# One kernel, two issue orders: a Newton-type matrix square root and a spectral convolution on one core

## The chip, the core and the metric

The kernel runs on one core of a Trainium2 chip. A core has five engines with instruction streams of their own: PE (TensorE, matrix products into the PSUM banks), DVE (VectorE), ACT (ScalarE), POOL (GpSimd) and SP (SyncE, which issues transfers here). They meet through semaphores. The metric is the time of one execution on the device in microseconds (us); lower is better.

## The reference

Input x is 32 images of 32 channels of 128 x 128 in float32. Cut to what matters:

```python
def _L0_conv_ref(A):                       # per image and channel, 128 x 128
    Y = A / norm(A);  Z = I
    for _ in range(5):
        T = 0.5 * (3 I - Z @ Y);  Y = Y @ T;  Z = T @ Z
    return Y * sqrt(norm(A))

def _L1_conv_ref(x, weights1, weights2):
    f = fftn(x, axes=(2, 3)).real
    top = einsum('bixy,ioxy->boxy', f[:, :, :32, :32], weights1)
    bot = einsum('bixy,ioxy->boxy', f[:, :, -32:, :32], weights2)
    return ifftn(zeros with top and bot put back).real

x = x + _L0_conv_ref(_gn(x))               # _gn: group norm, 16 groups of 2 channels
x = x + _L1_conv_ref(_gn(x), weights1, weights2)
```

## The kernel before, in words

**Layer 0.** The work unit is a *quad*, four channels of one image, 256 in all. `prep` takes the statistics of an image or a pair of images (bn_stats, L207, on the tiles `xs`), and from them the scales and offsets of the group norm; `root` (L152 to L162) takes square roots, and its last use in `prep`, with the tag `a_t`, makes the scale `a_t_s` of layer 0's result. `staged` normalizes a quad's input in two layouts, on ACT (L342) and POOL (L349). `newton` computes the root as a polynomial iteration of two `quartic` rounds. Each step is four products of 128 x 128 on PE (`products`, L308), a transposition on PE (L314) or a wide product (L418), and after it an evacuation of the PSUM bank: q, v, w, t by `plus` on DVE (L283), my, mb, t, y on ACT (L407, L410, L275, L421, L424), r = mb + eye on POOL (L295, L302). In images 1 to 18 (`is_far`) the transposed w comes another way: DVE turns blocks of v (L374), a transfer writes them to DRAM and another reads them back (L376, L384, L387), and POOL adds r (L389).

**Layer 1.** `settle` stores a finished quad, folds it on POOL (L441) and takes its statistics on DVE (L446). `forward` and `spectrum` transform an image, `wide_products` (L617, group of 20 images), `small_products` (L687, groups of 7 and 3) and `last_products` (L732, group of 2) multiply by the weights, mode by mode, and `inverse` transforms back and writes out: products L870, copies to SBUF L876, products L888, then ACT copies L900, DVE additions L905 and the sums L838 in `unfold`. In the groups of 7, 3 and 2 images the loaded products are first put in another order (L858 on ACT; L853 on ACT and DVE for the last two images). The products of a group read buffers `diag` and `plain` that have zeros outside the blocks; they are cleared on POOL (L604, L673, L709) before the group's loads on SP (L591, L593, L651, L657).

**The order of the work.** All of this is Python generators. A main loop runs *rounds*: in each it advances nine lanes, each a quad in `newton`, by one step, and in between one step of `prep`, of the posts (`settle`, `forward`), the spectra, the products and the inverses. `rest` and `pause` are two empty steps between a result and its use. So the source's own order interleaves independent chains. A scheduler then takes the traced instructions: it issues, engine by engine, by priority and by its own reckoning of what is ready, unless an instruction is pinned. `kept` (L184) is the scheduler's pin: the instruction is put behind the one that the source has just before it on its engine. Before, it is on all transfers, on the normalizations of `staged` and on the products of `forward`; all the rest may move.

## Time and profile before

| | |
|---|---|
| three runs | 3047.10, 3047.77 and 3060.30 us; median 3047.77 |
| the profiled execution | 3058.61 us; its span, first to last instruction, 3056.7 |
| granted TensorE clock, mean | 0.978 |
| instructions | 73392 |
| DMA | 636.40 MB, 208 GB/s on average |
| PE, products L308 and L418 | L308 with w and v: 4096 records, mean 279 ns; L418: 2048 records, mean 383 ns |
| DVE, L283 q | 512, mean 680 ns |
| DVE, bn_stats L207 and L446 | 512 each, mean 412 ns and median 418 ns |
| POOL, L389 and L441 | 288, mean 1276 ns; 512, mean 734 ns |

An engine's busy time is the time in which one of its instructions runs. A float32 product on PE leaves two records. The idle time of a group is the time in which its engine stood still just before its instructions, and the releaser is what ended that. The end of a matmul in the profile is modelled.

### The profile page before, as it was taken

How to read it: one execution, taken by the hardware profiler on the slowest of the kernel's cores; microseconds unless marked ns; L12 is line 12 of the kernel's file. 1: busy time of each engine (PE TensorE's matmuls, PEld its weight loads, DVE VectorE, ACT ScalarE, POOL GpSimd, SP SyncE). 2: the span in 40 equal slices, each digit the busy share in tenths (PEclk: the TensorE clock that was granted, in tenths of full speed). 3: DMA queues.
4: the chain of work that ended last, by engine and by line, in shares of the span. 5: the costliest groups of instructions: out<-in, count | busy, mean ns of one | idle time of the engine just before them, and what ended most of it. 6: DMA issues, size and time to landing. Idle time of an engine off the chain costs nothing.

```text
span 3056.7 us, 73392 instructions
## 1 busy us (share of the span) xinstructions
PE 2901.3 (95%) x27076; PEld 2697.1 (88%) x27076; DVE 2238.3 (73%) x4255; ACT 1638.1 (54%) x4187; POOL 1999.1 (65%) x2312
## 2 busy tenths in 40 slices
PE   6999999999999999999999999999899998999994
PEld 6899999999999999999999888898898887888883
DVE  6778787878787878777866545777777765867664
ACT  3566566566565566565545544454454444555552
POOL 4577777776767777777755435676676763777452
PEclk9999999999999999999999999999999998999996
DMA  5476766767576768676733666677667667665675
GB/s 168 159 229 209 218 210 219 222 204 226 187 231 194 242 193 247 186 245 189 232 101 115 190 199 223 204 247 241 205 216 247 219 232 231 205 205 199 194 242 202
DMA packets 476659, 636.40 MB, mean 208 GB/s; under 512 B 97040, under 2 KB 257296, under 8 KB 476304
## 3 DMA queue, kind: packets, MB, share of 16 engines
q1 hardware_dynamic: 362976, 424.31, 43.3%
q10 hardware_dynamic: 113328, 207.41, 21.7%
q8 instruction: 217, 3.56, 0.5%
q14 instruction: 138, 1.13, 0.1%
HBM read 402.42 MB, written 229.11 MB: 207 GB/s over the span
## 4 chain that ended last, share of the span: by engine, by line
PE 76%; DMA 11%; DVE 5%; POOL 3%; ACT 2%; issue 2%; SPq 1%; ACTq 0%; DVEq 0%; POOLq 0%
PE ps L308 50%; PE ps L418 12%; PE ps L314 6%; DMA xs<-in_xs 4%; PE ps L464 2%; DMA w<-turn 1%; PE ps L888 1%; DMA or<-od 1%; PE ps L617 1%; POOL yt L838 1%; PE ps L870 1%; PE ps L529 1%; DVE yt L905 1%; DMA plain<-in_wk 1%; DVE a_st L207 1%
## 5 line engine op out<-in xcount | busy, mean ns | idle before, releaser
L308 PE MATMUL ps<-w,v 128*128 128x128 f32 x4096 | 555.8, 279 | 16.3 <-POOL w L389 6.6
L389 POOL TENSOR_TENSOR w<-w,r 128x512 f32<-128x512 f32 x288 | 366.6, 1276 | 306.5 <-DMA w<-turn 249.5
L342 ACT ACTIVATE b<-b,a_off,a_sc 128x128 f32<-128x128 f32 x1024 | 467.3, 490 | 160.4 <-issue 48.0
L308 PEld LDWEIGHTS ps<-w,v 128*128 128x128 f32 x4096 | 507.6, 194 | 29.2 <-POOL w L389 8.3
L418 PE MATMUL ps<-my,q 128*128 128x256 f32 x2048 | 491.6, 383 | 9.6 <-ACT d L900 6.0
L441 POOL TENSOR_TENSOR fold<-xt 128x256 f32<-128x256 f32 x512 | 364.6, 734 | 170.2 <-DVE xt L428 155.9
L283 DVE SCALAR_TENSOR_TENSOR q<-ps,eye 128x512 f32<-128x512 f32 x512 | 348.2, 680 | 164.4 <-PE ps L308 158.3
L838 POOL TENSOR_TENSOR yt<-yt,d 128x512 f32<-128x512 f32 x248 | 310.5, 1282 | 197.2 <-ACT d L900 150.6
L418 PEld LDWEIGHTS ps<-my,q 128*128 128x128 f32 x2048 | 370.5, 191 | 56.6 <-ACT d L900 6.8
L349 POOL TENSOR_SCALAR x<-xt,a_nm,a_sc 128x128 f32<-128x128 f32 x736 | 324.1, 455 | 18.6 <-DVE a_n L234 18.6
L302 POOL TENSOR_TENSOR r<-mb,eye 128x512 f32<-128x512 f32 x112 | 142.8, 1275 | 295.5 <-ACT mb L275 282.3
L421 ACT ACTIVATE t<-ps 128x256 f32<-128x256 f32 x512 | 192.8, 383 | 231.4 <-PE ps L418 226.5
L424 ACT ACTIVATE y<-ps,a_t_s 128x128 f32<-128x128 f32 x1024 | 312.0, 370 | 0.0
L207 DVE BATCH_NORM_STATS2 a_st<-xs 128x6 f32<-128x256 f32 x512 | 195.8, 412 | 139.1 <-DMA xs<-in_xs 138.6
L308 PE MATMUL ps<-y,t 128*128 128x128 f32 x2048 | 276.5, 279 | 10.4 <-DVE t L283 9.6
L308 PE MATMUL ps<-x,q 128*128 128x128 f32 x2048 | 278.2, 279 | 6.2 <-DVE q L283 6.2
L308 PE MATMUL ps<-x,b 128*128 128x128 f32 x2048 | 277.9, 279 | 5.9 <-POOL x L349 5.7
L407 ACT ACTIVATE my<-ps 128x512 f32<-128x512 f32 x256 | 152.9, 597 | 243.0 <-PE ps L308 238.0
L308 PE MATMUL ps<-my,mb 128*128 128x128 f32 x2048 | 277.3, 279 | 3.1 <-ACT d L900 3.1
L308 PE MATMUL ps<-my,q 128*128 128x128 f32 x2048 | 277.7, 279 | 2.1 <-ACT my L407 2.1
L308 PE MATMUL ps<-q,t 128*128 128x128 f32 x2048 | 275.2, 278 | 1.2 <-ACT d L900 1.2
L308 PEld LDWEIGHTS ps<-my,q 128*128 128x128 f32 x2048 | 262.4, 194 | 14.6 <-issue 2.7
(138 smaller groups left out, 5572.4 us busy)
## 6 DMA issues: line engine op xcount, KB each, us to landing
turn<-turn SPq DMA_DIRECT2D x288, 256.0 KB
b<-in_x ACTq DMA_DIRECT2D x256, 256.0 KB
xt<-in_xt ACTq DMA_DIRECT2D x256, 256.0 KB
xs<-in_xs ACTq DMA_DIRECT2D x256, 256.0 KB
mid<-xt SPq DMA_DIRECT2D x256, 256.0 KB
yt<-mid SPq DMA_DIRECT2D x128, 512.0 KB
out<-yt SPq DMA_DIRECT2D x117, 512.0 KB
w<-turn SPq DMA_DIRECT2D x144, 256.0 KB
```

What stands on the lines that cost most here:

```text
L207: nc.vector.bn_stats(st[:, 2 * k + j, :], tiles[k][:, j, :])
L283: nc.vector.scalar_tensor_tensor(s, ps, f, t, ALU.mult, ALU.add)
L308: nc.tensor.matmul(ps[:, j, :], lhsT[:, j], rhs[:, j], start=True, stop=True)
L314: nc.tensor.transpose(ps[:, j, :], t[:, j, :], ident)
L342: nc.scalar.activation(t, x, AF.Identity, bias=offset[:, c], scale=scale[:, c])
L349: nc.gpsimd.tensor_scalar(m[:, j, :], xt[:, j, :], nm[:, c // 2 : c // 2 + 1], sc[:, c : c + 1], ALU.add, ALU.mult,)
L389: nc.gpsimd.tensor_tensor(w, w, r, ALU.add)
L418: nc.tensor.matmul(both[j // 2][:, j % 2], q[:, j], my[:, j], start=True, stop=True)
L421: nc.scalar.mul(w[:, 2 * h : 2 * h + 2, :], both[h][:, :, 1, :], 1 / (MS * QF))
L424: nc.scalar.mul(y[:, j, :], both[j // 2][:, j % 2, 0, :], sn[:, c : c + 1])
L441: nc.gpsimd.tensor_tensor(f[:, :, 64 * half : 64 * half + 64], xt[:, :, 0:64], xt[:, :, 64:128], op)
L838: engine.tensor_tensor(yh, yh, d, op)
```

## The change

Every engine is wrapped. Each instruction that the kernel issues through `nc` is pinned behind the one before it on its engine, so that all five streams stand in the order of the source. `kept` becomes a function that returns its argument, as the wrapper does its work already. The building of the identity (`make_identity`) goes on by the unwrapped handle. The result of the last root of layer 0 (`a_t_s`) gets three buffers in place of two. In a profile, an instruction issued through the wrapper shows the wrapper's line.

```diff
+class InOrder:
+    def __init__(self, tc):
+        self.tensor, self.vector, self.scalar, self.gpsimd, self.sync = (
+            Engine(tc, getattr(tc.nc, n)) for n in ("tensor", "vector", "scalar", "gpsimd", "sync")
+        )
+
+class Engine:
+    def __init__(self, tc, engine):
+        self.tc, self.engine = tc, engine
+
+    def __getattr__(self, name):
+        issue = getattr(self.engine, name)
+        def issued(*args, **kw):
+            return self.tc.keep_in_program_order(issue(*args, **kw))
+        return issued
...
-    nc = tc.nc
+    nc = InOrder(tc)
...
-    make_identity(nc, ident)
+    make_identity(tc.nc, ident)
...
-        s = small.tile([P, n], F32, tag=f"{tag}_s", name=f"{tag}_s", bufs=2)
+        s = small.tile([P, n], F32, tag=f"{tag}_s", name=f"{tag}_s", bufs=3 if tag == "a_t" else 2)
...
-    kept = tc.keep_in_program_order
+    def kept(issued):
+        return issued
```

## The prediction

> **What bounds the kernel now.** I read the engine totals first, then the 40 slices, then the same busy times for four stretches of the span.

> ```profile
> PE 2901.3 (95%) x27076; PEld 2697.1 (88%) x27076; DVE 2238.3 (73%) x4255; ACT 1638.1 (54%) x4187; POOL 1999.1 (65%) x2312
> ...
> PE   6999999999999999999999999999899998999994
> ...
> 0.00:200.00 200.00, 167.54 (x1334) 158.83 (x1335) 141.01 (x300) 100.40 (x251) 109.94 (x142) 0.98 0.54 173
> 200.00:1700.00 1500.00, 1494.24 (x12513) 1416.34 (x12512) 1196.06 (x2299) 881.93 (x2288) 1062.53 (x1197) 1.00 0.66 204
> 1700.00:2900.00 1200.00, 1133.48 (x12154) 1031.36 (x12153) 817.21 (x1503) 595.66 (x1506) 758.48 (x905) 0.97 0.67 217
> 2900.00:3057.00 157.00, 106.00 (x1083) 90.53 (x1081) 84.06 (x155) 60.12 (x145) 68.18 (x69) 0.82 0.68 225
> ```

> The columns are stretch, length, then busy time of PE, PEld, DVE, ACT and POOL, the granted clock, DMA share and GB/s. PE is the bound. Its idle time is 3056.7 - 2901.3 = 155.4 us: 32 us in the first 200 us (the start), 6 us in the next 1500, 67 us from 1700 to 2900 (where layer 1's products and inverse run beside layer 0), 51 us at the end. So the change can matter in two ways only: it shortens these 155 us, or it makes PE wait at new places.

> **The change part by part.** The lists of the built programs show which instructions move. SP's 1962 transfers stand in source order before and after. Of PE's 14,562 instructions, neighbours are out of order at 8 places, in the first round and around the small products (L687). ACT has 335 such places of 4973, POOL 310 of 2309, DVE 1011 of 4255. So PE keeps its order, and the question is whether its inputs come later or earlier. From the end of the input's last producer to the start of the product that reads it, the trace has a median of 3.3 to 5.4 us for every operand of the iteration (w from POOL 3.9, q 3.9 to 4.3, v 3.3) and a fifth percentile of 0.8 to 2.3. Shifts below 1 us are covered by that; larger ones are not.

> *(a) The copies L858.* The inverse of the images of groups 1 and 2 copies its loaded products on ACT and multiplies them on PE in the same step of the source. Before, most of these copies were issued 20 to 30 us early:

> ```profile
> 2599.24 2.01 ACT L858 COPY ob<-or 128x1024 f32<-128x1024 f32 x1
> ...
> 2621.33 1.65 ACT L342 ACTIVATE b<-b,a_off,a_sc 128x128 f32<-128x128 f32 x4 [0.36 <-issue]
> 2622.01 1.16 PE L870 MATMUL ps<-tab,ob 64*128 64x128 f32 x16
> ```

> The second copy (2599.24) feeds the products at 2622.01. In source order it stands behind the four L342 that end at 2622.98. The copy then ends at 2625.0, and PE, which reads nothing else first, waits 3.0 us. I did the same for all ten: end of the ACT instruction ahead in source order, plus 2.0 us, less the start of L870. The first copy of each group was late already and stays. The other eight give 3.0, 0, 2.7, 1.9, 3.0, 3.9, 2.7 and 3.0: 20 us. Nothing hides it but PE's own idle time, 6 us of 200 there. Bounds: 0 (ACT always ahead of PE) and 8 x 4 = 32. I take +20.

> *(b) The clears L604, L673, L709.* Before, POOL cleared the buffers of the products 53 us to over 600 us ahead; now each clear stands at the head of its stage, and the loads on SP wait for it, with all that SP has behind them.

> ```profile
> L604 POOL MEMSET diag<- x2: 1802/1804/1805, 1647.2 to 1650.4; 128x2048 f32 x2
> L604 POOL MEMSET plain<- x2: 943/944/944, 1652.1 to 1653.0; 128x1024 f32 x2
> ...
> 1696.87 3.35 SPq L591 DMA_DIRECT2D diag<-in_wk  x4
> 1700.25 1.27 POOL L302 TENSOR_TENSOR r<-b,eye 128x512 f32<-128x512 f32 x1 [0.63 <-POOL x L349]
> 1700.55 0.35 SPq L593 DMA_DIRECT2D plain<-xs  x1
> 1705.62 1.11 PE L617 MATMUL ps<-diag,plain 128*32 128x128 f32 x32 [1.01 <-DMA diag<-in_wk]
> ```

> POOL's instruction ahead in source order is the L302 that ends at 1701.5. Two clears of 1.80 and one of 0.94 end at 1706.1, so the load L593 goes out 5.5 us later than 1700.55, and the product, which waits for its loads already, starts 5.5 us later. For the small products I do the same. The first clear of the first stage ends at 2482.2 where its spectra went out from 2480.4 on, with products at 2486.4: 0 to 1.8, I take 1. In the second stage 2827.3 stands against 2826.1: 1.2. L709 moves by about 2 us, with 100 us until its buffers are used: 0. Together +8. Bounds: 0, and 16, the sum of the clears (5.5 + 3 x 3.6).

> *(c) The end.* The last image's two copies L853 ran on idle engines; in source order they follow image 30's evacuations.

> ```profile
> 3029.47 1.05 ACT L853 COPY ob<-or 128x512 f32<-128x512 f32 x1 [2.26 <-DMA or<-od]
> ...
> 3034.77 1.53 PE L870 MATMUL ps<-tab,ob 64*128 64x128 f32 x16
> ...
> 3039.35 0.97 ACT L900 COPY d<-ps 128x256 f32<-128x256 f32 x3 [0.34 <-DVE yt L905]
> ```

> The L900 end at 3040.3; the copy ends 1.05 later, at 3041.4, 6.6 us after 3034.77. Some returns, because the next product (L888 at 3040.86) had waited 4.6 us for ACT's other copies. +4, bounds 0 and 7.

> *(d) POOL's w (L389) behind r (L295).* Before, w stood ahead of an r that the source has first in 162 pairs, and POOL then stood waiting for w's transfer:

> ```profile
> L389 POOL TENSOR_TENSOR w<-w,r 128x512 f32<-128x512 f32 x288 | 366.6, 1276 | 306.5 <-DMA w<-turn 249.5
> ...
> PE ps L308 <- POOL w L389: 6.6, 3, 4.2
> ```

> Now r, 1.28 us, fills part of that wait and w comes later by what is left. I put POOL's rows in source order with their durations, and their inputs at the times at which they arrived. This makes w 1 us late on average, and where slack is short PE is late by 20 us in all. The turning transfer starts sooner in return: in the same accounting for DVE, L374 comes 0.4 us earlier, because bn_stats L446 (0.42 us each, 411 of 512 ran ahead of source order) no longer stand before it. Bounds -6 (the 6.6 us go away) and +20; I take +8.

> *(e) Order on DVE and ACT otherwise.* In favour: going through PE's waits of 0.3 us and more and adding up what had overtaken the late producer on its engine gives 22 us at most. Against: an instruction that waits now holds all behind it; the same accounting makes PE later by 20 us on DVE, over the accounting for the old order. I take -10, bounds -22 and +20, nearer the gain, because q, v, t and w themselves come 0.1 to 0.4 us earlier in it.

> *(f) The third buffer* of the root adds no instruction. The scale of an image pair is rewritten only once its last reader is done; before, the shortest distance was 1.0 us: 0.

> [...] The trace shows L870 at 2.08 us after 11.59 us idle against 1.16 at 2622.01. [...]

> **Sum.** 20 + 8 + 4 + 8 - 10 = +30 us on a span of 3056.7: 3087. The profiled execution took 3058.6, 10.8 us over the median of the runs, so I carry the difference to the median: 3047.8 + 30 = 3078. The ends of all bounds are -28 and +95; both at once is unlikely on either side.

> **The rivals.**
> 1. *The source order feeds PE better.* POOL and ACT no longer stand in front of transfers (249.5 us at L389, 23.2 at L858) and the critical instructions pass the statistics. Against: PE had only 6 us of idle between 200 and 1700 to give. It decides if (a) stays under 10 us and (e) reaches its 22: 3047.8 - 22 - 6 + 4 (half of b) + 4 (c) = 3028. Chance 0.22.
> 2. *Nothing is seen.* PE's order is the same and its slack of 4 us takes up the rest; losses in (a) come back as shorter waits later. Within 0.5% (15 us, about what a measurement can tell) of 3048: say 3052. Chance 0.18.
> 3. *One blocked head holds everything.* DVE waits 138.6 us for xs at L207 before; if such waits, with yt at L905, now stand before q and v all through 1700 to 2900, PE's 67 us of idle there double: 3078 + 67 = 3145. Against: L207 hardly moves in the lists. Chance 0.10.
> 4. *The wrapper misses calls.* It can't: all lists of after ascend in source order, but for one constant. Chance 0.

> The forecast itself has 0.50. Faster 0.22, within 0.5% 0.18, slower 0.60. The range runs from 3026, (e) at its good end and nothing lost elsewhere, to 3128: (a) and (c) as taken and the bad ends of (b), (d) and (e), 20 + 4 + 16 + 20 + 20 = 80.

> **What would show it.** L870 of the images 21 to 26, 28 and 29 waits 2 to 4 us for ob; the first L617 waits some 6 us for its loads; PE is 98 to 100% busy from 200 to 1700 still; POOL's idle before w falls below 250 us; DVE's bn_stats of xt come later. I am wrong if ACT reaches the copies before PE does, or if the stretch from 200 to 1700 loses more than 25 us.

## The result and the profile after

The changed kernel took 3069.23 us (median of 8 runs, 3062.66 to 3074.93), the kernel before beside it 3048.22 (8 runs, 3045.40 to 3060.30). The ratio is 1.0065, 95% interval [1.0048, 1.0083]: some 20 us slower, where 3078 was predicted. The total came out right, but two of its terms were off by 20 us and more, in opposite directions, so part of that is luck. That shows only where PE is followed through the stages.

The profile page of the changed kernel, engine totals and the 40 slices of PE:

```profile
span 3064.9 us, 73467 instructions
...
PE 2897.2 (95%) x27076; PEld 2689.8 (88%) x27076; DVE 2244.1 (73%) x4255; ACT 1644.0 (54%) x4187; POOL 1997.2 (65%) x2312
...
PE   6999999999999999999999999999999998899984
```

Its busy times by stretch, in the columns that the prediction explains:

```profile
0.00:200.00 200.00, 167.12 (x1333) 159.30 (x1334) 145.82 (x301) 99.93 (x251) 109.07 (x141) 0.99 0.55 173
200.00:1700.00 1500.00, 1471.63 (x12234) 1387.62 (x12233) 1179.17 (x2239) 865.33 (x2246) 1042.13 (x1172) 1.00 0.65 201
1700.00:2900.00 1200.00, 1146.68 (x12383) 1046.57 (x12382) 829.24 (x1554) 613.75 (x1537) 773.43 (x929) 0.98 0.68 220
2900.00:3065.00 165.00, 111.78 (x1132) 96.31 (x1131) 89.86 (x164) 64.95 (x154) 72.54 (x73) 0.82 0.66 216
```

From 200 to 1700 PE now stands still for 28 us (6 before). From 1700 to 2900 it stands still less, 53 us (67 before), and its clock is 0.98 against 0.97. So the stage that was full has lost and the stage with gaps has won.

How much, and where, comes from the starts of the same product in both traces, as PE issues its products in the same order in both:

| stretch, in times of before | delay of after at its end, us | change, us |
|---|---|---|
| 0 to 200 | 0 | 0 |
| 200 to 1570 | +32 | +32 |
| 1570 to 1870, the first L617 in it (1705.6) | +36 | +4 |
| 1870 to 2670 | -12 | -47 |
| 2670 to 2771, copies L858 | +2 | +14 |
| 2771 to 3056.7 | +8 | +6 |

The two profiled executions are only 8 us apart, the medians 21: that of before (3058.6) is 10 us over its median. So the single stretches are good to about 10 us, and the sizes are taken from the runs below. How far one execution can be trusted shows in four of them that have the same order up to 1620 (this one, e4, e6 and e7 below): their delays there are 32, 29, 44 and 36 us.

*The loss from 200 on: w behind a waiting r.* Groups of the page of after; all wrapped instructions show line L83, so they are told by their tiles:

```profile
L83 POOL TENSOR_TENSOR r<-mb,eye 128x512 f32<-128x512 f32 x256 | 326.5, 1275 | 431.6 <-ACT mb L83 413.3
...
L83 PE MATMUL ps<-w,v 128*128 128x128 f32 x4096 | 557.0, 279 | 34.3 <-POOL w L83 26.0
...
L83 POOL TENSOR_TENSOR r<-b,eye 128x512 f32<-128x512 f32 x256 | 326.4, 1275 | 214.7 <-ACT b L83 160.4
...
L83 POOL TENSOR_TENSOR w<-w,r 128x512 f32<-128x512 f32 x288 | 365.1, 1275 | 121.0 <-DMA w<-turn 94.8
```

POOL's idle time before w fell from 306.5 to 121.0 us, as predicted, but POOL did not stop waiting: it waits before r instead, for ACT's mb and b. The two groups of r here hold all images. By line, in the repetition e4_all_lines below, the r of images 1 to 18 (L295) has 201.5 us of idle time before it where it reads b and 112.4 where it reads mb, 314 together; the kernel before has 40. The other r (L302), with 319.6 us where it reads mb, belongs to images whose w does not run on POOL, and had 295.5 before. PE pays with 26.0 us of waits for w (6.6 before). Of 35 such waits, counted from 0.02 us up, 29 come where POOL had stood still before an r among the three instructions ahead of that w. One such place, in the timeline of after:

```profile
554.00 0.48 ACT L83 ACTIVATE b<-b,a_off,a_sc 128x128 f32<-128x128 f32 x1
...
554.61 1.27 POOL L83 TENSOR_TENSOR r<-b,eye 128x512 f32<-128x512 f32 x1 [3.65 <-issue]
...
555.84 2.50 POOL L83 TENSOR_TENSOR w<-w,r 128x512 f32<-128x512 f32 x2
...
557.17 1.16 PE L83 MATMUL ps<-w,v 128*128 128x128 f32 x8 [1.26 <-POOL w L83]
```

POOL stands for 3.65 us until ACT has normalized b, then runs r, and only then w, for which PE waits 1.26 us.

*The step at the first L617: clears ahead of loads.* Timeline of after:

```profile
1732.73 3.55 POOL L83 MEMSET diag<- 128x2048 f32 x2
...
1736.22 1.84 POOL L83 MEMSET plain<- 128x1024 f32 x2
...
1737.19 0.34 SPq L83 DMA_DIRECT2D plain<-xs  x1
...
1740.16 1.94 PE L83 MATMUL ps<-diag,plain 128*32 128x128 f32 x32 [3.60 <-DMA plain<-xs]
```

The load goes out (1737.19) only when the first clear of `plain`, 0.95 us from 1736.22 on, is done, and PE waits 3.60 us for it. The delay steps from +31.9 at 1670 to +37.4 at 1719. Only 2.6 us of this step are the later start of this product (+34.5, against 1705.62 before); the rest comes in 6.83 us at half clock from 1739.40 on.

*The copies.* Timeline of after, the products L870 of four images (start, duration, and in brackets PE's wait):

```profile
2613.36 2.08 PE L83 MATMUL ps<-tab,ob 64*128 64x128 f32 x16 [2.88 <-ACT ob L83]
...
2682.30 1.16 PE L83 MATMUL ps<-tab,ob 64*128 64x128 f32 x16 [2.60 <-ACT ob L83]
...
2750.54 1.94 ACT L83 COPY ob<-or 128x1024 f32<-128x1024 f32 x1
2752.53 1.25 PEld L83 LDWEIGHTS ps<-tab,ob 64*128 64x128 f32 x16 [3.71 <-ACT ob L83]
2752.53 1.54 PE L83 MATMUL ps<-tab,ob 64*128 64x128 f32 x16 [3.31 <-ACT ob L83]
```

PE waits for the end of the copy. The nine waits add up to 26.4 us (two waits and 5.9 us before). The same 16 products take 1.16 us after one wait, at a granted clock of 1.00 (2682.30), and 2.08 after another, at 0.50 (2613.36); the last section returns to that.

*The gain from 1870 on: DVE no longer stands in front of a transfer.* Timeline of the kernel *before*, the same stretch on three engines:

```profile
2323.83 0.68 DVE L283 SCALAR_TENSOR_TENSOR v<-my,ps 128x512 f32<-128x512 f32 x1
2329.41 0.43 DVE L207 BATCH_NORM_STATS2 a_st<-xs 128x6 f32<-128x256 f32 x1 [4.90 <-DMA xs<-in_xs]
2329.75 1.87 DVE L905 TENSOR_TENSOR yt<-ps,yt 128x512 f32<-128x512 f32 x3
2331.54 0.68 DVE L283 SCALAR_TENSOR_TENSOR w<-ps,r 128x512 f32<-128x512 f32 x1
...
2330.46 0.97 ACT L900 COPY d<-ps 128x256 f32<-128x256 f32 x3 [5.89 <-DVE yt L905]
...
2330.88 1.46 PE L418 MATMUL ps<-my,q 128*128 128x256 f32 x4 [3.55 <-ACT d L900]
```

The statistic L207 at 2329.41, which the source has later than the L905, the w and the L900 around it, stands at the head of DVE and waits 4.90 us for xs. Behind it wait L905, w, ACT's L900 (for L905) and PE (for the bank that L900 empties). The scheduler had issued 399 of the 512 L207 ahead of something that the source has earlier. From 1850 to 2650, the group of L207 in the kernel before:

```profile
L207 DVE BATCH_NORM_STATS2 a_st<-xs 128x6 f32<-128x256 f32 x128 | 49.6, 415 | 69.4 <-DMA xs<-in_xs 69.3
```

and in the changed kernel:

```profile
L83 DVE BATCH_NORM_STATS2 a_st<-xs 128x6 f32<-128x256 f32 x128 | 47.5, 413 | 4.6 <-DMA xs<-in_xs 4.5
```

The wait of 69.3 us is gone; whether that is the gain, the experiments tell.

### The profile page after: what moved, and what is told of

The parts are those of the page before. It is cut to its first block, busy times and chain, and to the rows that moved or that the text cites. A ratio compares the mean times of both kernels' runs of the same rounds, so it can differ in the third digit from the quotient of the medians.

```text
span 3064.9 us, 73467 instructions
## 1 busy us (share of the span) xinstructions
PE 2897.2 (95%) x27076; PEld 2689.8 (88%) x27076; DVE 2244.1 (73%) x4255; ACT 1644.0 (54%) x4187; POOL 1997.2 (65%) x2312
## 5 line engine op out<-in xcount | busy, mean ns | idle before, releaser
L83 PE MATMUL ps<-my,q 128*128 128x128 f32 (+1 forms) x4096 | 734.5, 329 | 3.2 <-DVE w L83 1.5
L83 PEld LDWEIGHTS ps<-my,q 128*128 128x128 f32 x4096 | 625.6, 191 | 61.1 <-issue 6.8
L83 POOL TENSOR_TENSOR r<-mb,eye 128x512 f32<-128x512 f32 x256 | 326.5, 1275 | 431.6 <-ACT mb L83 413.3
L83 PE MATMUL ps<-w,v 128*128 128x128 f32 x4096 | 557.0, 279 | 34.3 <-POOL w L83 26.0
L83 PEld LDWEIGHTS ps<-w,v 128*128 128x128 f32 x4096 | 504.9, 193 | 53.9 <-POOL w L83 34.9
L83 ACT ACTIVATE b<-b,a_off,a_sc 128x128 f32<-128x128 f32 x1024 | 469.6, 493 | 150.9 <-issue 45.8
L83 DVE SCALAR_TENSOR_TENSOR q<-ps,eye 128x512 f32<-128x512 f32 x512 | 350.9, 685 | 225.5 <-PE ps L83 219.8
L83 ACT ACTIVATE my<-ps 128x512 f32<-128x512 f32 x512 | 306.4, 603 | 377.9 <-PE ps L83 361.7
L83 POOL TENSOR_TENSOR r<-b,eye 128x512 f32<-128x512 f32 x256 | 326.4, 1275 | 214.7 <-ACT b L83 160.4
L83 POOL TENSOR_TENSOR fold<-xt 128x256 f32<-128x256 f32 x512 | 363.6, 732 | 128.5 <-DVE xt L83 126.6
L83 POOL TENSOR_TENSOR w<-w,r 128x512 f32<-128x512 f32 x288 | 365.1, 1275 | 121.0 <-DMA w<-turn 94.8
L83 POOL TENSOR_TENSOR yt<-yt,d 128x512 f32<-128x512 f32 x248 | 310.8, 1279 | 147.7 <-ACT d L83 110.4
L83 ACT ACTIVATE t<-ps 128x256 f32<-128x256 f32 x512 | 191.4, 381 | 373.4 <-PE ps L83 361.5
L83 POOL TENSOR_SCALAR x<-xt,a_nm,a_sc 128x128 f32<-128x128 f32 x736 | 322.6, 451 | 18.6 <-DVE a_n L83 18.6
L83 ACT ACTIVATE y<-ps,a_t_s 128x128 f32<-128x128 f32 x1024 | 290.4, 374 | 0.0
L83 PE MATMUL ps<-y,t 128*128 128x128 f32 x2048 | 276.9, 279 | 8.1 <-DVE t L83 5.8
L83 PE MATMUL ps<-x,b 128*128 128x128 f32 x2048 | 277.3, 279 | 5.7 <-POOL x L83 5.7
L83 PE MATMUL ps<-x,q 128*128 128x128 f32 x2048 | 275.7, 278 | 3.2 <-DVE q L83 3.2
L83 PE MATMUL ps<-my,mb 128*128 128x128 f32 x2048 | 276.9, 279 | 0.0
L83 PE MATMUL ps<-q,t 128*128 128x128 f32 x2048 | 274.8, 277 | 0.5 <-DVE u L83 0.5
L83 DVE STREAM_TRANSPOSE turn<-v 128x512 f32<-128x512 f32 x288 | 264.8, 919 | 9.9
L83 PEld LDWEIGHTS ps<-y,t 128*128 128x128 f32 x2048 | 254.8, 194 | 13.0 <-issue 6.6
```

What stands on the lines that cost most here:

```text
L83: return self.tc.keep_in_program_order(issue(*args, **kw))
```

## The experiments

All variants have the third buffer. Where an order is pinned, the same relation as in the change is added to the traced instructions of the named engines, so that the lines stay readable. Ratios are to the kernel before, run on the same chip (medians 3050.77 beside e1 to e4, 3049.08 beside e5 to e8 and 3052.90 beside e9 to e12); 1% is 30.5 us.

**One engine at a time, and all.**

```diff
+    in_order(('DVE',))                      # e1_dve
+    in_order(('Activation',))               # e2_act
+    in_order(('Pool',))                     # e3_pool
+    in_order(('PE', 'DVE', 'Activation', 'Pool', 'SP'))   # e4_all_lines
```

> Only DVE's stream stands in source order; ACT, POOL, PE and SP are as in the kernel before (third root buffer kept). Theory: what the changed kernel wins between the first inverse and image 24 (47 us by matching PE's products in the two traces: 27 us of PE idle time and 19 us of half-clock windows) comes from DVE's order, because statistics and additions no longer run ahead of q, v, t and w. Then about 3005 us (ratio 0.986). Rival A: it comes from ACT's order; then 3048 +- 8. Rival B: it needs DVE and ACT in order together; then 3048 +- 8 here and for ACT alone.

> Only ACT's stream in source order. Theory: the copies of the loaded products (L858) now stand right before the products that read them, PE waits for them 26 us in place of 6, nothing else changes: 3068 us (ratio 1.0065). Rival A (ACT's order also gives the 47 us of the middle): about 3021. Rival B: about 3068 as the theory; e1 then tells.

> Only POOL's stream in source order. Theory: w (L389) stands behind r (L295), which waits for ACT, and PE falls back by 32 us up to image 19; the clears (L604) cost 5.5 us more: 3048 + 37 = 3085 us (ratio 1.012). Rival: w is late only because ACT in order brings b and mb later, so POOL alone costs just the clears: 3054 (1.002).

> The changed kernel itself, pinned by a pass at the end of the trace instead of by a wrapper, so that each instruction keeps its own line in the profile: the same streams, 3069 us (ratio 1.0065) by every theory. It is the reference of this set, and shows by line what POOL's w and r wait for.

| run | median, us | ratio [95%] | in us |
|---|---|---|---|
| e1_dve | 3020.84 | 0.9892 [0.9874, 0.9911] | -33 |
| e2_act | 3077.63 | 1.0090 [1.0061, 1.0118] | +27 |
| e3_pool | 3064.47 | 1.0039 [1.0023, 1.0055] | +12 |
| e4_all_lines | 3071.44 | 1.0068 [1.0046, 1.0089] | +21 |

e4 repeats the changed kernel. The change is three changes: DVE's order wins, ACT's and POOL's lose. DVE's gain is three times the predicted one, though less than the 3005 expected of e1. ACT's loss goes with the copies: from 2570 to 2980, in times of before, PE stands still 16 us longer in e2. No run has ACT alone in order with the copies moved. PE's waits in e2:

```profile
PE ps L870 <- ACT ob L858: 25.5, 9, 3.7
PE ps L870 <- ACT ob L853: 17.8, 2, 11.5
```

POOL was expected at 3085 and reached 3064: that one missed. Its profile loses 21 us up to 1516 and wins 26 back after 1850. PE's idle time differs by 4 us there; it is the half clock that differs: from 1870 to 2980 the profiled execution of e3 has 17 us of it, that of before 72, and half of the difference is 27 us. That of e3 is the fastest of its nine (3057.30), that of before is 10 us over its median, so part of this is the choice of the executions. The three single effects add up to +6 against +21 together; the intervals reach 5 to 9 us to either side, so this hardly proves an interplay.

**Undoing one cost at a time, all five engines in order.** e5 makes r inside the quartic (ahead of its use, for images 1 to 18 behind the empty steps, after mb has long come), e6 puts one step between a copy and its products, e7 clears early, with further steps in the products' generators to find the room, e8 is all three.

```diff
-        ready.append((xt, m, mb, plus_eye(mb, is_far(b), has_more(b, g))))
+        ready.append((xt, m, mb))
...
             yield from rest
+            r = plus_eye(mb, far, more)
             w = four("w", more)
...
                     obs[b].rearrange("p (l t o) -> p o t l", l=4, t=8),
                 )
+            yield
...
-        for t in diags + plain:
-            nc.gpsimd.memset(t, 0.0)
...
+        for t in diags:
+            nc.gpsimd.memset(t, 0.0)
+        yield
```

> All five streams in source order, but the source makes r = mb + eye a rest (two rounds) later, inside the quartic, so that POOL reaches it when ACT has long written mb or b, and w no longer stands behind a waiting r. Theory (POOL's head-of-line wait at r makes w late): PE's waits for w fall from 26 us to under 8, and the 30 us lost up to image 19 come back: 3070 - 28 = 3042 us (ratio to before 0.998). Rival (w is late because of its own transfer or of POOL's load, 65% busy): PE's waits for w stay above 18 us, 3062 to 3070 us (1.005 to 1.007).

> All in source order, but in the inverse the copy L858 or L853 and the products L870 that read it are one step of the source apart. Theory: PE's waits for L858 fall from 26 us to under 4 and the time by about 20: 3050 us (ratio 1.001). Rival (the loss returns as other waits, for the inverse's own chain gets one step longer for 12 images): 3065 to 3075 us (1.006 to 1.009).

> All in source order, but the buffers of the products are cleared when they are made or a step after the last product of the group before, as the scheduler had it, not at the head of their own stage. Theory: only the first L617 gets back its wait, about 5.5 us: 3064 us (ratio 1.005). Rival (the clears hold SP's queue and with it later transfers): up to 15 us, 3055 us (1.002).

> All in source order with the three edits of e5, e6 and e7 together: r later, the copy a step ahead, the clears early. If the costs are separate, as the theory has it, they add: 3070 - 28 - 20 - 6 = 3016 us (ratio 0.990), below both the kernel before and the changed one, since DVE's gain stays. Rival (the costs hide behind one another): 3030 to 3045 us (0.994 to 0.999).

| run | median, us | ratio [95%] | against e4, us |
|---|---|---|---|
| e5_r_later | 3037.50 | 0.9964 [0.9948, 0.9980] | -32 |
| e6_copy_step | 3037.94 | 0.9961 [0.9948, 0.9973] | -33 |
| e7_clear_early | 3082.63 | 1.0120 [1.0094, 1.0147] | +16 |
| e8_three_edits | 3033.43 | 0.9949 [0.9934, 0.9964] | -36 |

e5 isolates r ahead of w. PE's waits for w in e4_all_lines:

```profile
PE ps L308 <- POOL w L389: 26.5, 31, 2.4
```

and in e5_r_later:

```profile
PE ps L308 <- POOL w L390: 7.2, 6, 2.4
```

At 1620 it is 9 us behind the kernel before, where e4 is 29 behind. Later runs make this firmer: the four executions with r ahead of w (the changed kernel, e4, e6 and e7) are 29 to 44 us behind at 1620, the four with r moved (e5, e8, e9 and e10) 2 to 9, though the other edits of e6 to e10 come into play later. So term (d) is some 30 us there, and 32 in the medians at the end. e6, expected at 3050, takes eight of the nine waits for L858 away (26.3 us in e4; one of 2.2 us is left in e6) and wins 33. From 2570 to 2980 it is 36 us shorter than e4: 22 of them are idle time of PE, and 10 are the clock, as it has 10 us at half rate there in place of 31. e7 missed. The step at the first L617 is smaller (+1.6 in place of +5.5), but e5, which leaves the clears where they are, has +1.4; and e7 loses about 7 us near 2200 and 6 near 2500, where the added steps move the inverses against the rest; it mixes two things and says little about clears. Its loss is inside e8 as well. e8 missed the 3016 of separate costs: it is 36 us below e4, where its three parts by themselves add up to 49.

**Only what has no side effect, and the end.** e9 has e5, e6 and the first clear (L604) moved to where `change` is entered, with no step added for it. e10 also issues image 31's copies L853 together with image 30's.

```diff
+        for t in diags + plain:            # in change(); gone from the wide products
+            nc.gpsimd.memset(t, 0.0)
...
+            if more:                       # e10 alone
+                load_products(b + 1)
+                for k in (b, b + 1):
...
+                    for h, copy in enumerate((nc.scalar.copy, nc.vector.tensor_copy)):
```

> Everything in the order of the source, with r made behind the rest, a step between the copy L858 and the products L870, and the first clear (L604) moved up to where change() is entered, with no other step shifted. If the three costs are separate, they come off one by one from the 3071 of e4_all_lines: 33 (r, e5_r_later), 33 (copies, e6_copy_step) and about 5 (first clear): 3001, a ratio of 0.985, with the delay against the kernel before near +9 at 1620, no step at the first L617, and about -65 at the end. If the costs hide behind one another (time won in the first layer's stage is given back in the second by whatever is next, as e8_three_edits hinted), 3015 to 3030, a ratio of 0.990 to 0.995.

> e9_three_fixed with the copies L853 of image 31 issued together with those of image 30, so ahead of image 30's last evacuations. If the last wait of the products for DVE ob (6.6 us) is a cost of its own, 4 to 6 us below e9_three_fixed; if what follows in the tail is set by the last loads and stores anyway, within 2 us of it.

e9: 3011.91 us (3003.61 to 3016.17), ratio 0.9870 [0.9842, 0.9898]; 60 us below e4, of 71 if all were separate. Its median lies above the 3001 of separate costs and below the rival's 3015 to 3030, nearer to neither for certain, as the interval is 9 us to either side. The delay against the kernel before is +2.3 at 1652, +1.6 at 1859, -54.0 at 2662, -55.7 at 2973: the first stage and the copies cost next to nothing now, and the gain of the middle stays. What follows gives 8 back, PE's wait in the tail being longer (11.6 and none before):

```profile
PE ps L872 <- ACT ob L854: 19.6, 1, 19.6
...
PE ps L872 <- DVE ob L854: 6.2, 1, 6.2
```

e10: 3008.14 us, ratio 0.9861 [0.9827, 0.9895]. The wait for DVE ob is gone from its list, but the profiled span is 3011.9 against 3009.2, and the intervals overlap almost whole. What remains in the tail is a wait of 18.8 us for ACT ob, and ACT had itself stood 10.34 us for the load of `or`. Whether e10 gains 4 us can't be told from these runs.

**Where DVE's gain comes from.** e11 is the kernel before with only the statistics pinned (L207, shown, and L446 in the same way), e12 is e1 with r made later.

```diff
-                nc.vector.bn_stats(st[:, 2 * k + j, :], tiles[k][:, j, :])
+                kept(nc.vector.bn_stats(st[:, 2 * k + j, :], tiles[k][:, j, :]))
```

> The kernel before with the third buffer, and of all instructions only the statistics L207 and L446 kept in the order of the source on DVE. If what DVE's order wins (e1_dve, -33) is that statistics no longer run ahead of the roots' and evacuations' work, 3018 to 3025, a ratio of 0.990 to 0.993, with the delay against the kernel before turning from about +5 to below -20 between 1817 and 2620. If the gain is in the order of the other DVE operations (q, v, t, w, the preparations), 3045 to 3052, a ratio within 0.3% of 1.

> Only DVE in the order of the source (as e1_dve, 3021), with r made behind the rest as in e5_r_later. If the +10 that e1_dve shows at 1817 comes from r ahead of w, about 3010, a ratio of 0.986, with the waits of L308 for POOL w at 7 us or less, from 14.3; if those 10 us come from DVE w (11.8 us in e1_dve), no change: 3018 to 3023.

e11: 3017.65 us (3012.26 to 3030.47), ratio 0.9902 [0.9864, 0.9941], -30 us: as much as the whole order of DVE in e1, with 1024 pinned instructions. The delay goes from +6 at 1859 to -34 at 2559. The two rows of DVE from 1850 to 2650 and of PE's clock that go with it, in e11:

```profile
L207 DVE BATCH_NORM_STATS2 a_st<-xs 128x6 f32<-128x256 f32 x128 | 47.7, 412 | 2.9 <-DMA xs<-in_xs 2.8
```
```profile
1850.00:2650.00 800.00, 768.86 (x7653) 702.40 (x7653) 609.42 (x1128) 415.56 (x1069) 571.63 (x669) 0.99 0.72 237
```

and in the kernel before:

```profile
1850.00:2650.00 800.00, 747.89 (x7279) 681.14 (x7278) 573.22 (x1065) 392.19 (x1015) 540.40 (x631) 0.96 0.69 227
```

In 800 us PE is busy 21 us more, at 0.99 of its clock in place of 0.96. So the gain is that statistics no longer run ahead; the order of q, v, t and w among themselves is not needed for it. L207 and L446 were not pinned apart; the waits are L207's.

e12: 3038.18 us, ratio 0.9962 [0.9946, 0.9979]. Neither reading expected it to be slower than e1. PE's waits for w are the same (13.7 us, 14.3 in e1): so moving r in the source changed nothing in them while POOL's order is the scheduler's. Why e12 is 17 us above e1 stays open; its delay is +12 at 457 already, where e1 has +3, and a change of the source gives the scheduler other orders on all engines that are not pinned.

## Why the prediction was right, point by point

**(a) Copies, +20: right in its mechanism, short by the clock.** For the eight copies behind the first of their group PE waited 2.88, 0.03, 2.60, 2.46, 3.31, 3.69, 2.53 and 3.31 us, where 3.0, 0, 2.7, 1.9, 3.0, 3.9, 2.7 and 3.0 were forecast; the two first ones waited 5.6 us, 5.9 before. That is the forecast nearly copy by copy. The step that fell short: it has no term for the clock. Six of the nine waits were followed by a granted clock of 0.50, five times for 3.41 us and once for 6.83; half of these 23.9 us is 12 us, an estimate. Taking the waits out won 33 us (e6).

**(b) Clears, +8: the first number was met by luck.** The step of 5.5 us at the first L617 is there, but it is made up otherwise. The load L593 went out 4.7 us later against the products around it (5.5 forecast), and the product only 2.6. The forecast took it that the product "waits for its loads already", but the wait of 1.01 us was for `diag`; the load of `plain` had, by these figures, some 2 us to spare. The other 2.9 us come in the half clock behind it. Nor does the step belong to the clears alone: with the clears early, as in the kernel before, e2, e11 and e12 show 4.3, 3.0 and 3.2 us there and e10 shows 3.2; with the clears at the head of the stage e5 shows 1.4. So the 0.1 of e9 does not size the clear, and the small ones were not isolated either (e7).

**(c) The end, +4: the wait is there, its price is not settled.** Timeline of after:

```profile
3043.95 1.11 ACT L83 COPY ob<-or 128x512 f32<-128x512 f32 x1
3044.50 1.45 DVE L83 COPY ob<-or 128x512 f32<-128x512 f32 x1
...
3046.09 2.08 PE L83 MATMUL ps<-tab,ob 64*128 64x128 f32 x16 [6.60 <-DVE ob L83]
```

The wait is the 6.6 us of the forecast; the whole tail moved by about 2 us.

**(d) r ahead of w, +8: right in its mechanism, mis-sized beyond its bound of 20.** The trace of after shows 32 us lost from 200 to 1570, and moving r away wins 32 (e5). As far as the runs show, the step that failed is the discount from the 20 us of the accounting to 8, because the turning transfer "starts sooner in return". With DVE alone in source order PE's waits for w did not fall, they rose from 6.6 to 14.3 us (e1); and with POOL alone in order the delay at 1516 is 21 us (e3), near the 20 without the discount. The accounting also took the inputs "at the times at which they arrived". If w is late on PE, mb and b may come late from ACT in turn; that was not tested. The own words "if the stretch from 200 to 1700 loses more than 25 us" came true here. In the medians POOL's order by itself costs 12 us, clears and all (e3).

**(e) Order on DVE and ACT otherwise, -10: mis-sized, beyond its bound of -22.** e1 and e11 give -33 and -30. The step that failed counted what had *overtaken* a late producer, by its busy time. A statistic that overtakes costs 0.41 us of work, but it also stands and waits for its transfer, 69 us from 1850 to 2650. The clock had no term either: from 1870 to 2500 the profiled execution of after is 44 us shorter than that of before, 26 of them idle time of PE and 17 from 34 us less at half clock; as that of before is 10 us over its median, the clock's part may be smaller in the medians. The reason given against rival 3, that "L207 hardly moves in the lists", was wrong: 399 of 512 did. Rival 3's blocked head was there, but in the kernel before.

**(f) The third buffer** is in all variants alike; it was not tried by itself.

By engine the forecast was ACT +24 (a and c), POOL +16 (b and d) and DVE -10; the engines one at a time gave +27, +12 and -33. By themselves ACT and POOL were sized well, and DVE was wrong by 23 us. Together they came to +21 and not +6; why is open, if it is more than noise. In company (d) was too small by 24 us and (a) by 13, and (e) by 23 the other way. That these cancel as far as they do is luck, and they are not separate costs: 33, 32 and -33 alone add up to 32, more than the 21 us measured. Rival 1, the source order feeding PE better, is what DVE's order does by itself, and e9 shows it for all five queues once r and the copies are out of the way.

## What to carry to other kernels

Pinning an order is one decision for each queue, not one (here -33 us for DVE, +27 for ACT, +12 for POOL): ask of each queue which instruction waits longest, and what stands behind it. An instruction that waits for a transfer or for another engine belongs late in its queue, and an early place for work that nobody needs soon (statistics of the next images) costs by its wait, not by its busy time alone: from 1850 to 2650 the wait at L207 fell from 69.4 to 2.9 us in e11, its busy time only from 49.6 to 47.7. Here pinning 1024 statistics alone gave 1% (e11), and the source order with r and the copies moved gave 1.3% (e9), where the plain source order loses 0.65%.

## What the runs showed of the hardware

In these traces the clock fell at short waits of PE. From 200 to 2980 us, the kernel before has 18 stretches at half clock (0.50), of 3.41 or 6.83 us, each at a wait of 1.6 to 5.8 us or just after it. Four waits over 1.7 us had none after them. A wait and what follows it, in the windows of after (clock in the third column from the end):

```profile
2749.20:2752.50 3.30, 0.02 (x1) 0.00 (x0) 0.00 (x0) 3.22 (x6) 1.55 (x2) 1.00 1.06 326
2753.20:2756.60 3.40, 3.40 (x22) 3.18 (x19) 0.48 (x1) 1.07 (x2) 0.00 (x0) 0.50 1.02 305
2757.00:2760.00 3.00, 3.00 (x30) 3.00 (x28) 2.00 (x3) 2.22 (x6) 1.99 (x3) 1.00 0.79 281
```

The prediction has no term for this. The mean clock of a stretch hides it: from 1700 to 2900 the kernel before has 12 such windows of 3.41 us and 4 of 6.83, together 68.3 us at half rate, or 34 of 1200 us, which *is* its 0.97.

```profile
2678.07:2681.48 3.41, 1.63 (x15) 1.39 (x14) 2.58 (x4) 3.01 (x7) 1.03 (x1) 1.00 1.07 335
2681.48:2684.89 3.41, 2.59 (x29) 2.47 (x30) 3.16 (x5) 2.17 (x5) 3.41 (x5) 1.00 0.21 65
2715.62:2719.03 3.41, 0.95 (x16) 0.79 (x16) 0.69 (x1) 2.57 (x3) 3.37 (x4) 1.00 0.95 233
2719.03:2722.44 3.41, 3.41 (x21) 3.19 (x18) 0.69 (x1) 1.07 (x2) 3.34 (x6) 0.50 1.08 396
```

From 200 to 2980 us in after, the clock fell from full to half after 12 steps of the grid, in which PE was idle for 1.90 to 2.98 of 3.41 us, and stayed full after all other steps at full clock, of which the emptiest had 1.91. In before it fell after 18 steps, idle for 1.62 us and more, and stayed full up to 1.71. In these two traces the border thus lies somewhere between 1.6 and 1.9 us of idle time in one step. Where a wait fell on the grid told the two above apart, not which was longer.
